# Layer 0 of a two-layer image kernel: two normalising products moved from VectorE to GpSimd

## The chip, the cores and the metric

The kernel runs on one core of one Trainium2 chip. The metric is device time in microseconds (us) of one execution of the whole program: the median of three runs of the kernel before is 8276.61 us (8267.24 to 8282.14).

## The reference, cut to what matters

Two layers, each a mixer and then a small quantised feed-forward network, on an image `x` of shape (2, 96, 96, 96): batch, channel, row, column. The change lies in the mixer of layer 0, in two of its normalisations:

```python
def _ln_c(v, eps=1e-6):                     # over the 96 channels
    m = jnp.mean(v, axis=1, keepdims=True)
    s = jnp.var(v, axis=1, keepdims=True)
    return (v - m) / jnp.sqrt(s + eps)

x = x + _L0_conv_ref(_ln_c(x), ...)
# inside _L0_conv_ref
xz = einsum('bchw,ec->behw', x, in_proj_w)  # xin (192 channels) and a gate z
x_s = grid_sample_bilinear(xin, ...)        # offsets from a 3x3 convolution of xin
...                                         # four directions, each:
    hst = hst * dA + (dt * ut) * bt         # selective scan over windows of 36, 16 states
    y = einsum('bkdn,bkn->bkd', hst, ct)
mu = y.mean(-1); var = ((y - mu) ** 2).mean(-1)            # over 192 channels
y = (y - mu) * rsqrt(var + 1e-05) * ln_gamma + ln_beta
return einsum('bhwd,od->bohw', y * silu(z), out_proj_w)
```

The norm of `x` (the first function) and the norm of `y` (over the 192 channels after the scan) are what the change touches.

## The kernel before

Layer 0 walks over 32 stripes (2 images, 16 stripes of 6 rows, so T = 576 positions, H2 = 288 the half of them). For each stripe there is a front (`_l0_front`, line 488), a scan (`_l0_scan`, 1013, and `_l0_section`, 1055) and a back (`_l0_back`, 936). While stripe n is scanned, the front of stripe n+1 and the back of stripe n-1 are slipped in between.

The front normalises 8 rows of `x` in two column blocks of 384 (`norm`, from line 532): TensorE subtracts the mean (L534), ScalarE squares into `sq` and copies the centred values into `xc` (L538, L539), TensorE averages the squares into the PSUM tile `va` (L542), ScalarE turns them in place into reciprocal deviations by Ln and Exp (L548, L549), and VectorE multiplies `xc` by `va` into `xn` (L552). TensorE then projects `xn` (L557). The rest of the front is the convolution, the interpolation on GpSimd (14 sums and products a stripe, L681 to L687), and the step sizes of the scan, with four GpSimd products each (L810 to L813). The temporaries of the front come from five buffers with the tag "g".

The scan has 64 units for each stripe, 2048 in all. A unit is: TensorE spreads B over the partitions into the PSUM tile `bp` (L1104), VectorE multiplies it by `dur` (L1108), VectorE runs the scan into a state tile `h` in SBUF (L1125), GpSimd multiplies `h` by the replicated C, `cre` (L1130), and TensorE folds the states into `y` (L1143). ScalarE makes the decays `dA` for two units at a time (L1088). There are six state tiles `h`, two `bp` and two `dA`. The first product of every pair of units waits also for the GpSimd product and the fold of the unit whose state tile comes free (`wait` in `unit`).

The back centres `y` (L956 on TensorE; L966 and L967 on ScalarE write the squares `ysq` and the tile `Y`), averages the squares into a PSUM tile `yva`, takes the reciprocal deviation in place on ScalarE (`_power`, L862 and L863), and VectorE multiplies both halves of `Y` by it, 96x576 elements an instruction, two instructions a stripe (L975). GpSimd multiplies `Y` by the gate `zs` (L984), TensorE projects and adds the input (L994, L998), and a feed-forward network follows (`_plan_ffn`), with a VectorE product of its own (L894) and a GpSimd sum at the end (L932). The temporaries of the back, [96, 576] each, come from two buffers with the tag "b".

The order of the instructions is not written out by hand. `_Plan` takes every operation with its engine, a planned cost (`_cost`, by engine and columns, in RATE), its dependences, its buffers and a due time, and lays the operations out in a list order for each engine; `_in_order` then fixes this order. Due times of the scan come from a planned 3.4 us a unit, those of front and back are spread between two such points (`_dues`). Where the plan leaves TensorE idle, it fills in small matmuls without effect (`keep` in `_layer0`, L1188), so many for each gap. An operation that moves from one engine to another changes the plan, and so the order on all engines. Layer 1 follows when layer 0 has ended, with plans of its own.

Of the kernel before, what the change touches and what calls it, by code (L numbers as in the profile page):

```python
# [13 lines left out]
AF = mybir.ActivationFunctionType  # L14
ALU = mybir.AluOpType
# [11 lines left out]
C = 96  # L27
HW = 96
# [4 lines left out]
T = WIN * HW  # L33
H2 = T // 2
# [74 lines left out]
class _Plan:  # L109
# [19 lines left out]
    def op(self, eng, cost, run, r=(), w=(), due=0.0, tab=None, also=(), scan=False, first=False):  # L129
        o = _Op(eng, cost * self.rate.get(eng, 1.0), run, due, tab)  # L130
        o.scan, o.first = scan, first
        ref = lambda t: t if isinstance(t, tuple) else (t, None)
        meets = lambda a, b: a is None or b is None or a == b
        for t, key in map(ref, r):
            o.deps.update(p for p, q in t.writes if meets(key, q))
        for t, key in map(ref, w):
            o.deps.update(p for p, q in t.writes + t.reads if meets(key, q))
        for t, key in map(ref, r):
            t.reads.append((o, key))
        for t, key in map(ref, w):  # L140
            t.writes.append((o, key))
        o.deps.discard(o)
        for t in [x[0] for x in map(ref, list(r) + list(w))] + list(also):
            if t not in o.tiles:
                o.tiles.append(t)
        for t in o.tiles:
            if not t.users and t.tag != "p":
                t.queue.append(t)
            t.users.append(o)
        self.ops.append(o)  # L150
        return o
# [323 lines left out]
def _cost(S, eng, cols):  # L475

    fixed, each = (RATE if S.fine else LOOSE)[eng]
    return fixed + each * cols


def _op(S):
    def op(eng, n, run, r, w, also=(), tab=None, times=1):
        S.op(eng, times * _cost(S, eng, n), run, r, w, also=also, tab=tab)

    return op


def _l0_front(k, P, S, f, x, b, s, at):
# [3 lines left out]
    nc = k.nc  # L492
# [4 lines left out]
    temp = lambda shape, name, skip=0: S.tile(P.front, shape, "g", P.ng, name=name, skip=skip)  # L497
# [4 lines left out]
    def pe(cols, run, r, w, also=()):  # L502
        S.op("pe", _cost(S, "pe", cols), run, r, w, also=also)

    def act(cols, run, r, w, tab=None, times=1):
        S.op("act", times * _cost(S, "act", cols), run, r, w, tab=tab)

    def dve(cols, run, r, w):
        S.op("dve", _cost(S, "dve", cols), run, r, w)
# [17 lines left out]
    pool(8, lambda: nc.gpsimd.memset(xin.ap[:, :, :, 1 : HW + 3 : HW + 1], 0.0), (), (xin,))  # L527
    rows = lambda t, c: t.ap[:, 4 * c : 4 * c + 4, :].rearrange("p r w -> p (r w)")
    N4 = 4 * HW
    xc, sq, xn = temp([C, 8, HW], "axc"), temp([C, 8, HW], "asq"), temp([C, 8, HW], "xn")  # L530

    def norm(c):
        pc, va = ps("axc"), ps("ava")
        pe(N4, lambda: nc.tensor.matmul(  # L534
            pc.ap[:C, :N4], k.less_mean, rows(xt, c), start=True, stop=True), (xt,), (pc,), (xc,))

        def centred():
            nc.scalar.activation(rows(sq, c), pc.ap[:C, :N4], AF.Square)  # L538
            nc.scalar.copy(rows(xc, c), pc.ap[:C, :N4])  # L539

        act(N4, centred, (pc,), ((xc, c), (sq, c)), times=2)
        pe(N4, lambda: nc.tensor.matmul(  # L542
            va.ap[:C, :N4], k.mean96, rows(sq, c), start=True, stop=True),
            ((sq, c),), (va,), (xn,))

        def power():
            v = va.ap[:C, :N4]
            nc.scalar.activation(v, v, AF.Ln, bias=k.eps6[:C])  # L548
            nc.scalar.activation(v, v, AF.Exp, scale=-0.5)  # L549

        act(N4, power, (), (va,), tab="e", times=2)
        dve(N4, lambda: nc.vector.tensor_tensor(  # L552
            rows(xn, c), rows(xc, c), va.ap[:C, :N4], ALU.mult), ((xc, c), va), ((xn, c),))

    def project(half, c):
        pi, n = ps("pi"), PART[half]
# [7 lines left out]
    for c in range(2):  # L564
        norm(c)
# [282 lines left out]
def _dues(S, n0, at):  # L848

    ops = S.ops[n0:]  # L850
    whole, sofar = sum(o.cost for o in ops), 0.0
    for o in ops:
        o.due = at(sofar / whole)
        sofar += o.cost


def _power(k, op, v, eps, out=None):

    v_ = lambda: v.ap[:C, :H2]

    def run():
        k.nc.scalar.activation(v_(), v_(), AF.Ln, bias=eps[:C])  # L862
        k.nc.scalar.activation(v_() if out is None else out.ap, v_(), AF.Exp, scale=-0.5)  # L863

    op("act", H2, run, (), (v,) if out is None else (v, out), tab="e", times=2)
# [70 lines left out]
def _l0_back(k, P, S, f, ffn, res, dst, at):  # L936

    nc = k.nc
    n0 = len(S.ops)
    Y, zs = f.Y, f.zs  # L940
    temp = lambda name: S.tile(P.back, [C, T], "b", 2, name=name)
    ps = lambda name: S.tile(P.ps, [128, 512], "p", P.np, name=name)
    cols = lambda c: slice(c * H2, (c + 1) * H2)

    op = _op(S)
    xr = S.tile(P.back, [C, T], "xr", 1)
    S.op("sp", 1.2, lambda: nc.sync.dma_start(
        xr.ap.rearrange("p (i w) -> p i w", w=HW), res), (), (xr,))
    x1, sq = xr, [temp("ysq"), temp("ysq2")]

    def both(w, src, name, r):

        out = ps(name)

        for half in range(2):
            op("pe", H2, lambda half=half: nc.tensor.matmul(  # L956
                out.ap[:C, :H2], w(half), src(half), start=(half == 0), stop=(half == 1)),
                r, (out,))
        return out

    def centred(c):
        pc = [both(lambda half, h=h: k.less_mean192 if half == h else k.minus_mean192,
                   lambda half: Y.ap[:, half, cols(c)], "yc", ((Y, c),)) for h in range(2)]
        for h in range(2):
            def run(h=h):
                nc.scalar.activation(sq[h].ap[:, cols(c)], pc[h].ap[:C, :H2], AF.Square)  # L966
                nc.scalar.copy(Y.ap[:, h, cols(c)], pc[h].ap[:C, :H2])  # L967

            op("act", H2, run, (pc[h],), ((sq[h], c), (Y, c)), times=2)

    def normed(c):
        va = both(lambda half: k.mean192, lambda half: sq[half].ap[:, cols(c)], "yva",
                  ((sq[0], c), (sq[1], c)))
        _power(k, op, va, k.eps5)
        op("dve", 2 * H2, lambda: nc.vector.tensor_tensor(  # L975
            Y.ap[:, :, cols(c)], Y.ap[:, :, cols(c)],
            va.ap[:C, :H2].unsqueeze(1).to_broadcast([C, 2, H2]), ALU.mult),
            (va,), ((Y, c),))

    for c in range(2):  # L980
        centred(c)
        normed(c)
    for h in range(2):
        op("pool", T, lambda h=h: nc.gpsimd.tensor_tensor(  # L984
            Y.ap[:, h], Y.ap[:, h], zs.ap[:, h], ALU.mult), (zs,), (Y,))

    def project(c):
        pp = ps("pp")

        half = slice(c * HW // 2, (c + 1) * HW // 2)  # L990
        img = lambda t: t.ap.rearrange("p (i w) -> p i w", w=HW)[:, :, half].rearrange(
            "p i (w j) -> p w i j", j=WIN)

        op("pe", H2, lambda: nc.tensor.matmul(  # L994
            pp.ap[:C, :H2], k.ident[:C, :C], img(x1), start=True, stop=False), (Y, zs, (x1, c)), (pp,))
        for n, (w, v) in enumerate(((k.w_outb, zs), (k.w_out, Y))):
            for h in range(2):
                op("pe", H2, lambda n=n, w=w, v=v, h=h: nc.tensor.matmul(  # L998
                    pp.ap[:C, :H2], w[:, h, :], v.ap[:, h, cols(c)],
                    start=False, stop=(n == 1 and h == 1)), (v,), (pp,))  # L1000
        op("act", H2, lambda: nc.scalar.copy(
            img(x1), pp.ap[:C, :H2].rearrange("p (w i j) -> p w i j", i=WIN, j=WIN)),
            (pp,), ((x1, c),))

    for c in range(2):
        project(c)

    x2 = _plan_ffn(k, S, op, ps, temp, P.back, 1, ffn, x1)
    S.op("sp", 1.2, lambda: nc.sync.dma_start(dst, x2.ap), (x2,), ())
    _dues(S, n0, at)  # L1010
# [152 lines left out]
def _layer0(k, tc, a, x, x2d):  # L1163
# [3 lines left out]
    with ExitStack() as st:  # L1167
# [29 lines left out]
        def front(n):  # L1197
            if n < len(stripes):
                t0, t1 = (64 * n - 90) * tau, (64 * n - 12) * tau
                _l0_front(k, P, S, F[n], x, *stripes[n], lambda v: t0 + v * (t1 - t0))  # L1200

        def back(n):
            b, s = stripes[n]
            t0, t1 = (64 * n + 68) * tau, (64 * n + 135) * tau
            _l0_back(k, P, S, F[n], ffn, x[b, :, s * WIN : (s + 1) * WIN, :],
                     x2d[b, :, s * T : (s + 1) * T], lambda v: t0 + v * (t1 - t0))
# [834 lines left out]
```

## Time and profile before

| what | us |
|---|---|
| median of three runs | 8276.61 |
| the profiled execution, its own time | 8276.3 |
| its span in the trace | 8274.5 |
| first scan to last scan of layer 0 | from 149 to 6227 |
| VectorE busy in the span | 7653.1 (92%) |
| TensorE busy | 7337.5 (89%) |
| ScalarE busy | 6308.6 (76%) |
| GpSimd busy | 5188.3 (63%) |
| TensorE clock granted, mean | 0.959 |

PE is TensorE, PEld its weight loads, DVE VectorE, ACT ScalarE, POOL GpSimd. A group's line names the source line, the engine and the operation, output and inputs with their shapes, how often it ran, its busy time and the mean duration of one in ns, and then the idle time of that engine just before, with what ended it. Busy time counts overlapping instructions of an engine once. The shares over the whole span mix two stages: layer 0, in which GpSimd works all the time, and layer 1, after some 6260 us, in which it hardly works.

### The profile page before, as it was taken

Reading aid. Unit: us, or ns where it says so; the run is one execution under the profiler, and the core shown is the slowest. Engines: PE = TensorE matmul, PEld = TensorE weight load, DVE = VectorE, ACT = ScalarE, POOL = GpSimd, SP = SyncE. Lnnn points to the kernel's source line nnn. Section 1 sums busy time; section 2 is a strip of 40 time slices with the busy share of each in tenths; the row PEclk is TensorE's granted clock in tenths of the full one; section 3 lists DMA queues with packets and bytes.
Section 4 is the critical chain, followed back from the end, with each engine's and each line's share of the span. In section 5 each row is a group of like instructions: output and inputs, shape, how many; then the busy total and the mean of one; then the engine's idle time right before and its main releaser. Section 6 shows DMA issues by size and latency. Waiting matters only on the chain. (4 is left out here: it accounts for less than half of the span.)

```text
span 8274.5 us, 124621 instructions
## 1 busy us (share of the span) xinstructions
PE 7337.5 (89%) x46413; PEld 3261.5 (39%) x46413; DVE 7653.1 (92%) x5404; ACT 6308.6 (76%) x10654; POOL 5188.3 (63%) x3835
## 2 busy tenths in 40 slices
PE   7888888888888888888888888988878999989998
PEld 3333344434334333434443433433334223532245
DVE  3999999999999999999999999999996998969988
ACT  5777777778777887877777787778756886778867
POOL 4888888888888888888888888888862000110001
PEclk8999998999999999999999999999999999989999
DMA  3445544544545454454545454454441000110001
GB/s 93 159 156 156 157 151 155 156 151 156 157 153 158 156 166 153 153 159 155 155 150 157 150 157 156 155 159 158 154 132 47 3 3 20 33 47 3 2 22 33
DMA packets 359853, 992.25 MB, mean 120 GB/s; under 512 B 69288, under 2 KB 71680, under 8 KB 359040
## 3 DMA queue, kind: packets, MB, share of 16 engines
q1 hardware_dynamic: 357440, 984.04, 38.3%
q8 instruction: 367, 6.01, 0.3%
q14 instruction: 254, 2.08, 0.1%
q10 hardware_dynamic: 1792, 0.12, 0.0%
HBM read 797.19 MB, written 139.25 MB: 113 GB/s over the span
## 5 line engine op out<-in xcount | busy, mean ns | idle before, releaser
L1130 POOL TENSOR_TENSOR h<-h,cre 128x864 f32<-128x864 f32 x2048 | 3475.2, 1713 | 957.4 <-DVE h L1125 639.7
L1125 DVE TENSOR_TENSOR_SCAN h<-dA,bp 128x864 f32<-128x864 f32 x2048 | 3900.6, 1939 | 51.2 <-PE y L1143 30.6
L1088 ACT ACTIVATE dA<-dlr,A 128x576 f32<-128x576 f32 x3072 | 2157.9, 765 | 892.8 <-DVE h L1125 839.8
L1108 DVE TENSOR_TENSOR bp<-dur,bp 128x864 f32<-128x864 f32 x2048 | 2082.2, 1048 | 187.9 <-PE bp L1104 81.4
L1143 PE MATMUL y<-h,fold 128*32 128x288 f32 (+2 forms) x18432 | 1789.7, 436 | 229.6 <-POOL h L1130 202.1
L1143 PEld LDWEIGHTS y<-h,fold 128*32 128x32 f32 x18432 | 738.8, 114 | 963.4 <-POOL h L1130 674.8
L1503 ACT ACTIVATE pr<-sc 128x960 f32<-128x960 f32 (+1 forms) x1080 | 954.0, 937 | 200.1 <-PE sc L1499 179.2
L1104 PE MATMUL bp<-bt,selb 128*128 128x288 bf16 x2048 | 615.6, 301 | 508.4 <-DVE h L1125 491.2
L1583 DVE TENSOR_TENSOR sums<-sums,pr 128x3840 f32<-128x3840 f32 (+1 forms) x240 | 959.1, 3996 | 55.7 <-ACT pr L1503 33.7
L1675 POOL MEMSET vch<- 96x32 f32 x16 | 2.4, 153 | 1319.7 <-DVE dist L1537 1210.1
L1104 PEld LDWEIGHTS <-selb 128*128 128x128 bf16 x2048 | 198.9, 97 | 1200.9 <-DVE h L1125 1006.3
L1499 PE MATMUL sc<-qH,kH 32*128 32x480 f32 (+1 forms) x3240 | 627.4, 602 | 9.6 <-issue 5.0
L1188 PE MATMUL y<-selb,minus 128*32 128x288 bf16 x3528 | 605.7, 295 | 0.0
L1499 PE MATMUL sc<-q,kH 32*128 32x480 f32 (+1 forms) x1080 | 564.6, 602 | 0.0
L1565 PE MATMUL av<-pr,vT 128*32 128x480 f32 (+1 forms) x4320 | 533.4, 564 | 3.7 <-ACT av L1590 3.5
L1756 DVE SCALAR_TENSOR_TENSOR acc<-vch,lepe_w,acc 96x1152 f32<-96x1152 f32 x320 | 466.2, 1457 | 8.4 <-ACT vch L1691 0.4
L1188 PEld LDWEIGHTS <-minus 128*32 128x32 bf16 x3528 | 298.0, 98 | 225.6 <-issue 131.2
L1499 PEld LDWEIGHTS sc<-qH,kH 32*128 32x128 f32 x3240 | 219.6, 184 | 419.8 <-issue 220.6
L617 PE MATMUL pc<-xin,w_ca 128*128 128x288 f32 x1152 | 365.1, 423 | 1.2 <-ACT xin L560 1.2
L932 POOL TENSOR_TENSOR x<-x,fy 96x576 f32<-96x576 f32 x32 | 52.9, 1653 | 461.4 <-ACT fy L931 372.4
L791 PE MATMUL pt<-xd,w_dt 96*128 96x288 f32 x768 | 280.7, 455 | 7.3 <-ACT r L797 4.4
L810 POOL TENSOR_TENSOR e<-e,du 128x576 f32<-128x576 f32 x192 | 231.1, 1204 | 60.0 <-ACT du L806 59.7
(284 smaller groups left out, 10961.8 us busy)
## 6 DMA issues: line engine op xcount, KB each, us to landing
cre<-c_d SPq DMA_DIRECT2D x1024, 288.0 KB, 3.5
dur<-du_d SPq DMA_DIRECT2D x256, 864.0 KB, 5.6
dlr<-dl_d SPq DMA_DIRECT2D x256, 864.0 KB, 5.1
x<-xs SPq DMA_DIRECT2D x512, 72.0 KB, 2.4
du_d<-du SPq DMA_DIRECT2D x128, 288.0 KB, 2.5
dl_d<-dl SPq DMA_DIRECT2D x128, 288.0 KB, 2.6
du_d<-du SPq DMA_DIRECT2D x128, 144.0 KB, 2.5
dl_d<-dl SPq DMA_DIRECT2D x128, 144.0 KB, 2.4
```

The lines of the kernel that those rows point to most:

```text
L1088: nc.scalar.activation(dA.ap[:, :, blk, :], dlr.ap[:, blk, :].rearrange("p (c n) -> p c n", c=2), AF.Exp, scale=k.A[:, i, kg, h, blk : blk ...
L1104: nc.tensor.matmul(bp.ap[:, :H2], k.selb[:, kk, i, :], f.bc[o].ap[:, toks], start=True, stop=True)
L1108: nc.vector.tensor_tensor(bp.ap[:, : NBL * H2].rearrange("p (b n) -> p b n", b=NBL)[:, ::-1], dur.ap[:, ::-1, toks], bp.ap[:, :H2].unsquee ...
L1125: nc.vector.tensor_tensor_scan(hv, dv, bv, 0.0, ALU.mult, ALU.add)
L1130: nc.gpsimd.tensor_tensor(ht.ap, ht.ap, cre.ap[:, toks].unsqueeze(1).to_broadcast([128, NBL, H2]), ALU.mult)
L1143: nc.tensor.matmul(dst, k.fold, v, start=start, stop=stop)
L1188: nc.tensor.matmul(P.awake.ap[NBL * CB :, T - HEAD + 2 * 72 : HEAD], k.minus[:, :CB], k.selb[:, 0].rearrange("p i m -> p (i m)")[:, : HEAD ...
L1499: nc.tensor.matmul(two[to // 2][:, to % 2, :n], kH[rows, k0 : k0 + 128], q, start=True, stop=True)
L1503: nc.scalar.activation(pr[:, 2 * i : 2 * i + 2, :n], two[i][:, :, :n], AF.Exp, scale=HD**-0.5)
L1565: nc.tensor.matmul((main if s < HEADS else other)[s * HD : (s + 1) * HD, :n], vT[:, blk, hd, :], pr[:, place(s, p), :n], start=at == 0, st ...
L1583: nc.vector.tensor_tensor(both, both, pr[:, :, :, :n], ALU.add)
L1756: S.op("dve", 1.43, lambda: nc.vector.scalar_tensor_tensor(acc.ap, src(), W.lw[:, t : t + 1], acc.ap, ALU.mult, ALU.add), (vch,), (acc,))
```

## The change

In the front, the Exp no longer writes to the PSUM tile but to the SBUF tile of the squares `sq` (which the mean has read by then), and the product is issued on GpSimd, from `xc` and `sq`. `sq` gets a start that is two floats into its buffer. In the back the same is done with `sq[0]` and `Y`; `_power` is written out as a function of its own there. The back's temporaries have three buffers in place of two, and start two floats into theirs.

```diff
-    xc, sq, xn = temp([C, 8, HW], "axc"), temp([C, 8, HW], "asq"), temp([C, 8, HW], "xn")
+    xc, sq, xn = temp([C, 8, HW], "axc"), temp([C, 8, HW], "asq", 2), temp([C, 8, HW], "xn")
...
             nc.scalar.activation(v, v, AF.Ln, bias=k.eps6[:C])
-            nc.scalar.activation(v, v, AF.Exp, scale=-0.5)
-
-        act(N4, power, (), (va,), tab="e", times=2)
-        dve(N4, lambda: nc.vector.tensor_tensor(
-            rows(xn, c), rows(xc, c), va.ap[:C, :N4], ALU.mult), ((xc, c), va), ((xn, c),))
+            nc.scalar.activation(rows(sq, c), v, AF.Exp, scale=-0.5)
+
+        act(N4, power, (), (va, (sq, c)), tab="e", times=2)
+        pool(N4, lambda: nc.gpsimd.tensor_tensor(
+            rows(xn, c), rows(xc, c), rows(sq, c), ALU.mult), ((xc, c), (sq, c)), ((xn, c),))
...
-    temp = lambda name: S.tile(P.back, [C, T], "b", 2, name=name)
+    temp = lambda name: S.tile(P.back, [C, T], "b", 3, name=name, skip=2)
...
-        _power(k, op, va, k.eps5)
-        op("dve", 2 * H2, lambda: nc.vector.tensor_tensor(
+        rs = lambda: sq[0].ap[:, cols(c)]
+
+        def power():
+            nc.scalar.activation(va.ap[:C, :H2], va.ap[:C, :H2], AF.Ln, bias=k.eps5[:C])
+            nc.scalar.activation(rs(), va.ap[:C, :H2], AF.Exp, scale=-0.5)
+
+        op("act", H2, power, (), (va, (sq[0], c)), tab="e", times=2)
+        op("pool", 2 * H2, lambda: nc.gpsimd.tensor_tensor(
             Y.ap[:, :, cols(c)], Y.ap[:, :, cols(c)],
-            va.ap[:C, :H2].unsqueeze(1).to_broadcast([C, 2, H2]), ALU.mult),
-            (va,), ((Y, c),))
+            rs().unsqueeze(1).to_broadcast([C, 2, H2]), ALU.mult),
+            ((sq[0], c),), ((Y, c),))
```

## The prediction, made before the result

> **What bounds the kernel now.** I read the page's slices first: GpSimd is busy to about 6250 us, which is layer 0; after that the changed lines don't run. So only layer 0 matters, and I took the stretch from its first scan to its last (149 to 6227 us) for all further views. The busy times of that stretch:
>
> ```profile
> core 0: us, PE busy (x) PEld busy (x) DVE busy (x) ACT busy (x) POOL busy (x), PEclk, DMA share, GB/s
> 149.00:6227.00 6078.00, 5297.41 (x34108) 2420.51 (x34106) 5896.27 (x4278) 4695.65 (x8119) 5019.07 (x3605) 0.96 0.49 154
> ```
>
> DVE is busy 5896.3 of 6078 us (97%), and idle for 182 us. POOL is busy 83%, PE 87%, of which 605 us are the filling matmuls of L1188. 6078 / 2048 units is 2.97 us a unit. The groups of DVE in this stretch:
>
> ```profile
> L1125 DVE TENSOR_TENSOR_SCAN h<-dA,bp 128x864 f32<-128x864 f32 x2048 | 3900.6, 1939 | 51.2 <-PE y L1143 30.6 <-ACT dA L1088 9.9 <-POOL bot L687 1.6
> L1108 DVE TENSOR_TENSOR bp<-dur,bp 128x864 f32<-128x864 f32 x2046 | 2080.2, 1048 | 137.9 <-PE bp L1104 81.4 <-POOL h L1130 27.8 <-ACT dA L1088 6.3
> L975 DVE TENSOR_TENSOR Y<-Y,yva 96x576 f32<-96x576 f32 x62 | 45.4, 732 | 0.8 <-ACT yva L863 0.8
> L552 DVE TENSOR_TENSOR xn<-axc,ava 96x384 f32<-96x384 f32 x60 | 31.6, 531 | 0.0
> L894 DVE TENSOR_TENSOR fxq<-fxc,fva 96x288 fp8e5<-96x288 f32 x62 | 26.7, 433 | 0.0
> ```
>
> The reader is to see that the two products the change removes hardly ever wait (0.8 us): they stand in a full queue and push the scan back by their own length. Who makes DVE wait, and who makes POOL wait:
>
> ```profile
> DVE bp L1108 <- PE bp L1104: 81.4, 106, 2.6
> DVE h L1125 <- PE y L1143: 30.6, 26, 4.7
> DVE bp L1108 <- POOL h L1130: 27.8, 40, 1.9
> ...
> POOL h L1130 <- DVE h L1125: 639.7, 367, 6.9
> ```
>
> POOL waits for DVE far more than DVE for POOL: POOL is the follower. The chain of waits of the last stripe says the same (products and scans of DVE, no POOL until the scans are over). The groups of POOL that price the new work:
>
> ```profile
> L1130 POOL TENSOR_TENSOR h<-h,cre 128x864 f32<-128x864 f32 x2047 | 3473.5, 1713 | 957.3 <-DVE h L1125 639.7 <-PE y L1143 81.5 <-issue 34.3
> L984 POOL TENSOR_TENSOR Y<-Y,zs 96x576 f32<-96x576 f32 x62 | 74.2, 1203 | 0.0
> L932 POOL TENSOR_TENSOR x<-x,fy 96x576 f32<-96x576 f32 x32 | 52.9, 1653 | 461.4 <-ACT fy L931 372.4 <-DVE acc L1756 59.9 <-ACT fva L862 15.6
> ```
>
> **What the Trainium skill says.** GPSIMD Engine Reference, section 3.1, puts a float32 tensor_tensor at 1.96 times VectorE's time. The trace agrees roughly: 1203 ns for 96x576 on POOL against 732 ns on DVE, 1.64 times. PSUM — Partial Sum Buffer, section "The four PSUM rules", says that GpSimd cannot touch PSUM: so the Exp must write to SBUF before POOL can take the product; in the trace no POOL group has a PSUM operand. SBUF — State Buffer, section "Who interferes with whom", says that a VectorE instruction with two SBUF inputs blocks, or is blocked by, a GpSimd instruction that reads SBUF, and one with a single SBUF input isn't. In layer 0 every DVE product and scan has one input in PSUM, and the scan took 1917 to 1971 ns in all its 2048 runs, with POOL working or not: agrees. The change brings no DVE instruction with two SBUF inputs. ScalarE: Activation LUTs, section "What ACT_TABLE_LOAD costs", has 1283 ns for a load (plus a drain, which I can't see in the trace); the trace shows 1283.
>
> **The change part by part**, against the profiled execution's own time of 8276.3 us (span 8274.5), which is the median of the runs within 0.3 us.
>
> (a) *Removed from DVE.* 64 products of `xn` and 64 of `Y`; 60 and 62 of them are recorded in the stretch, 31.6 + 45.4 = 77.0 us. Neighbours on DVE overlap: the durations add up to 2048 x 1.939 + 2046 x 1.048 + 77.0 + 26.7 = 6218.9 us, the busy time is 5896.3, so each of the 4278 instructions hides 75 ns. Freed: 77.0 - 122 x 0.075 = 68 us. All of it lies on the path, since DVE is full.
>
> (b) *Lost overlap.* A scan that follows straight on its own product can't overlap it. The timeline shows both cases:
>
> ```profile
> 3010.51 3.79 DVE L1125 TENSOR_TENSOR_SCAN h<-dA,bp 128x864 f32<-128x864 f32 x2
> 3014.22 1.04 DVE L1108 TENSOR_TENSOR bp<-dur,bp 128x864 f32<-128x864 f32 x1
> 3015.29 1.95 DVE L1125 TENSOR_TENSOR_SCAN h<-dA,bp 128x864 f32<-128x864 f32 x1
> 3017.16 2.00 DVE L1108 TENSOR_TENSOR bp<-dur,bp 128x864 f32<-128x864 f32 x2
> 3019.07 3.79 DVE L1125 TENSOR_TENSOR_SCAN h<-dA,bp 128x864 f32<-128x864 f32 x2
> 3022.78 2.00 DVE L1108 TENSOR_TENSOR bp<-dur,bp 128x864 f32<-128x864 f32 x2
> ```
>
> A single unit takes 3017.16 - 3014.22 = 2.94 us, a pair 3022.78 - 3017.16 = 5.62, or 2.81 a unit. In the compiled order such scans number 233 before and 278 after, because removed products had stood between the two: 45 x 0.13 = +6 us.
>
> (c) *Added to POOL.* `Y` by the row of L984: 64 x 1.20 = 77 us. A 96x384 product isn't in the trace; between 1203 ns for 576 and 662 ns for a 96x288 product of layer 1 (L1283) it is 0.84: 54 us. Together 131 us, or 4.1 a stripe. From both sides: not under 0.66 a piece for `xn` (the smaller shape), and not over 1.65 for either (L932 in layer 1, where it met other DVE work): 119 to 211 us. POOL idles for 1059 us in the stretch, so the mean has room; what decides is bunching. I added up the order's heaviest runs with these prices: 12 units in a row cost POOL 38.7 us before and 39.9 after at most, against 12 x 2.97 = 35.6 for DVE; 32 units 91.3 and 93.9 against 95. POOL falls some 4 us behind either way, which six state tiles (six units, 17.8 us) cover. Cover that is gone shows as waits of DVE for POOL; those, and the waits for the fold behind it, are 27.8 + 30.6 = 58 us now. POOL's idle share falls from 17.4% to about 14.5%; if waits grow in inverse ratio, 58 x (17.4 / 14.5 - 1) = +12 us. This term is a choice; its ends are -20 (the new order happens to meet fewer waits) and +40.
>
> (d) *A wait moved.* The POOL products wait for ScalarE's Exp, and behind them on POOL stand state products, for which PE's folds and then DVE wait. On DVE the same wait cost 0.8 us in 122 instructions; the plan puts the product behind the Exp. I take zero, hidden by the state tiles; at worst 128 waits of the longest seen there (0.8) make 102 us on POOL, within its idle time.
>
> (e) *ScalarE.* Exp writes SBUF in place of PSUM: 387 ns for 96x288 into PSUM (L863), 387 for the copy of the same shape from PSUM into `Y` in SBUF (L967): zero. The order has 378 table loads against 360: 18 x 1.28 = 23 us on an engine with 1382 idle us there; zero on the path. The PSUM tile comes free a product earlier, the squares' tiles later; the third buffer of the back covers the latter. Zero.
>
> (f) *PE.* 3146 filling matmuls against 3528, 382 fewer of 0.29 us: 110 us less on PE, but they fill gaps only. Zero. SP's queue carries the same DMAs, none is added, and POOL issues none.
>
> (g) *Ends.* Before the first scan, `xn` comes later by 0.84 - 0.55 = 0.3 us. After the last scan the chain runs Exp, product, two gate products: the second Exp ends at 6237.07, two POOL products of 1.2 end by about 6238.65 and the gate by 6241.05, against 6240.30: +0.8 us.
>
> Sum: -68 + 6 + 12 + 1 = -49; 8276.3 - 49 = 8227 us.
>
> **The rivals.**
> *More than that:* the replanned order also meets fewer waits (PE's queue is lighter by the filling). With (c) at -20 and (b) at zero: -68 - 20 + 1 = -87, 8189. For it: 112 of the 182 idle us are waits for PE. Against: nothing was done about them.
> *PE takes over:* the freed time turns into waits for `bp` of L1104, since PE is busy 87% and is the latest releaser already (81.4 us). It would give 8270 to 8280, say 8274. For it: PE's work is unchanged and packed closer. Against: PE waits for DVE's scans before most of these matmuls, and 605 us of its busy time is filling.
> *Slower, by GpSimd's bunching:* the added 131 us lie in the queue ahead of state products, at the places where POOL is already behind (interpolation, step sizes); each delays the release of a state tile, and DVE stops. If all of it reached DVE: -68 + 6 + 131 + 1 = +70, 8346; with three quarters, 8313. It decides from 68 - 7 = 61 us, 47% of the added time. For it: POOL's rows of 1.2 us come in runs. Against: 40 waits for POOL in 2046 products.
> That the change doesn't do what it says is out: the compiled order has 128 DVE instructions fewer and 128 POOL ones more.
>
> **How the numbers follow.** About 0.2% of 8276, 16 us, is what the measurement can tell from no change. Forecast (8200 to 8255) 0.57; more than that 0.16; PE takes over 0.15, of which a third still ends below 8260; slower by bunching 0.12, of which a quarter ends within 16 us. Faster: 0.57 + 0.16 + 0.05 = 0.78; same 0.10 + 0.03 = 0.13; slower 0.09. The range goes from the low end of the second case (8180) into the third case (8278).
>
> **What would show it.** Right: the stretch of the scans is 45 to 90 us shorter, DVE's idle time there stays near 190 us, L975 and L552 appear on POOL at 1.2 and 0.84 us, and layer 1 is as long as before. Wrong: waits of DVE for POOL over 90 us (bunching), for L1104 over 130 (PE), POOL products at twice their price, or scans longer than 1.95 us.

## The result, and the profile after

The changed kernel takes 8160.81 us, the median of four runs (8149.47 to 8167.62), against 8272.03 us for the kernel before in the same comparison: a ratio of 0.9863, 95% interval 0.9845 to 0.988, so 111 us less. The forecast was 8227 us with a range from 8180. The sign was right, the gain was more than twice the 49 us forecast, and the time lies below the range. The profiled execution, the fastest of the four, has a span of 8147.7 us, 126.8 less than the one before.

The line numbers of the changed kernel are six higher from the back on: the product `bp` is L1114, the scan L1131, the state product L1136, the spread L1110, the fold L1149. First the stretch from the first scan to the last, with the busy time of each engine:

```profile
core 0: us, PE busy (x) PEld busy (x) DVE busy (x) ACT busy (x) POOL busy (x), PEclk, DMA share, GB/s
148.00:6095.00 5947.00, 5212.03 (x33725) 2369.59 (x33723) 5821.53 (x4156) 4713.82 (x8137) 5130.13 (x3727) 0.97 0.50 157
```

The stretch is 131 us shorter (6078 before). DVE's busy time fell by 74.7 us (5896.3 before), and its idle time by 56 (181.7 before, 125.5 now). So the gain has two parts of similar size. POOL carries 111 us more. The groups of DVE, and the new ones of POOL, in this stretch:

```profile
L1131 DVE TENSOR_TENSOR_SCAN h<-dA,bp 128x864 f32<-128x864 f32 x2048 | 3900.0, 1939 | 61.4 <-PE y L1149 39.9 <-ACT dA L1094 7.2 <-POOL bot L686 1.7
L1114 DVE TENSOR_TENSOR bp<-dur,bp 128x864 f32<-128x864 f32 x2046 | 2073.4, 1046 | 71.2 <-PE bp L1110 24.1 <-PE y L1149 17.2 <-ACT dA L1094 12.2
L894 DVE TENSOR_TENSOR fxq<-fxc,fva 96x288 fp8e5<-96x288 f32 x62 | 26.8, 432 | 0.0
...
L981 POOL TENSOR_TENSOR Y<-Y,ysq 96x576 f32<-96x576 f32 x62 | 74.6, 1204 | 0.0
...
L552 POOL TENSOR_TENSOR xn<-axc,asq 96x384 f32<-96x384 f32 x60 | 51.8, 864 | 0.0
```

The scan's mean didn't move (1939 ns), and the two products cost POOL what was forecast (1204 and 864 ns, against 1.20 and 0.84). Who makes DVE wait, in us, times and longest, and below it POOL's first wait:

```profile
DVE h L1131 <- PE y L1149: 39.9, 39, 2.9
DVE bp L1114 <- PE bp L1110: 24.1, 44, 1.7
DVE bp L1114 <- PE y L1149: 17.2, 21, 1.7
...
DVE bp L1114 <- POOL h L1136: 2.2, 9, 0.4
...
POOL h L1136 <- DVE h L1131: 507.5, 308, 5.6
```

DVE waited 81.4 us for the spread matmul before and 24.1 now; for POOL's state product 27.8 and 2.2. Both were expected to stay or grow. The wait for the folds grew, from 33.4 to 57.1 (two lines each). So the wait for POOL and for the folds behind it is nearly the same in sum, and the fall of the idle time is as large as the fall of the wait for the spread matmul. Busy time is explained by the products that left. The experiments ask where the 56 us of idle time went.

### The profile page after: what moved, and what is told of

It reads as the page before. It is cut to its first block, busy times and chain, and to the rows that moved or that the text cites. A ratio compares the mean times of both kernels' runs of the same rounds, so it can differ in the third digit from the quotient of the medians.

```text
span 8147.7 us, 123836 instructions
## 1 busy us (share of the span) xinstructions
PE 7250.8 (89%) x46031; PEld 3210.3 (39%) x46031; DVE 7575.8 (93%) x5276; ACT 6328.2 (78%) x10672; POOL 5305.7 (65%) x3963
## 5 line engine op out<-in xcount | busy, mean ns | idle before, releaser
L1136 POOL TENSOR_TENSOR h<-h,cre 128x864 f32<-128x864 f32 x2048 | 3481.2, 1714 | 753.5 <-DVE h L1131 507.5
L1131 DVE TENSOR_TENSOR_SCAN h<-dA,bp 128x864 f32<-128x864 f32 x2048 | 3900.0, 1939 | 61.4 <-PE y L1149 39.9
L1114 DVE TENSOR_TENSOR bp<-dur,bp 128x864 f32<-128x864 f32 x2048 | 2075.4, 1046 | 188.4 <-DMA dur<-du_d 117.3
L1149 PE MATMUL y<-h,fold 128*32 128x288 f32 (+2 forms) x18432 | 1790.0, 434 | 221.7 <-POOL h L1136 198.7
L1149 PEld LDWEIGHTS y<-h,fold 128*32 128x32 f32 x18432 | 725.9, 113 | 974.9 <-POOL h L1136 669.5
L1110 PE MATMUL bp<-bt,selb 128*128 128x288 bf16 x2048 | 613.5, 300 | 458.7 <-DVE h L1131 440.4
L1110 PEld LDWEIGHTS <-selb 128*128 128x128 bf16 x2048 | 197.3, 96 | 1163.0 <-DVE h L1131 956.4
L1194 PE MATMUL y<-selb,minus 128*32 128x288 bf16 x3146 | 552.0, 301 | 0.0
L1194 PEld LDWEIGHTS <-minus 128*32 128x32 bf16 x3146 | 274.0, 100 | 212.5 <-issue 122.3
L932 POOL TENSOR_TENSOR x<-x,fy 96x576 f32<-96x576 f32 x32 | 53.2, 1662 | 461.1 <-ACT fy L931 387.7
L791 PE MATMUL pt<-xd,w_dt 96*128 96x288 f32 x768 | 264.2, 440 | 7.7 <-ACT r L797 4.8
```

Of the source, the lines that this page charges most:

```text
L1110: nc.tensor.matmul(bp.ap[:, :H2], k.selb[:, kk, i, :], f.bc[o].ap[:, toks], start=True, stop=True)
L1114: nc.vector.tensor_tensor(bp.ap[:, : NBL * H2].rearrange("p (b n) -> p b n", b=NBL)[:, ::-1], dur.ap[:, ::-1, toks], bp.ap[:, :H2].unsquee ...
L1131: nc.vector.tensor_tensor_scan(hv, dv, bv, 0.0, ALU.mult, ALU.add)
L1136: nc.gpsimd.tensor_tensor(ht.ap, ht.ap, cre.ap[:, toks].unsqueeze(1).to_broadcast([128, NBL, H2]), ALU.mult)
L1149: nc.tensor.matmul(dst, k.fold, v, start=start, stop=stop)
L1194: nc.tensor.matmul(P.awake.ap[NBL * CB :, T - HEAD + 2 * 72 : HEAD], k.minus[:, :CB], k.selb[:, 0].rearrange("p i m -> p (i m)")[:, : HEAD ...
```

## The experiments

Times are medians; "idle" is DVE's in the stretch from 148 us to the end of the last scan, one profiled execution each. The kernel before was run beside every group, at 8270 to 8282 us, and the ratio is to those runs, taken from all runs and not from the two medians. A difference in us between kernels of two groups is uncertain by these 12 us.

| kernel | us | ratio to before (95%) | DVE busy | idle |
|---|---|---|---|---|
| before | 8272.0 | 1 | 5896 | 183 |
| changed | 8160.8 | 0.9863 (0.9845 to 0.988) | 5822 | 125 |
| e1 old order, product on POOL | 8360.0 | 1.0099 (1.0076 to 1.0122) | 5838 | 332 |
| e2 held plan, product on DVE | 8327.6 | 1.0059 (1.0039 to 1.0079) | 5904 | 247 |
| e3 held plan, product on POOL | 8295.7 | 1.0019 (1.001 to 1.0027) | 5846 | 266 |
| e4 before, less filling | 8276.9 | 1.0004 (0.9993 to 1.0016) | 5896 | 185 |
| e5 front alone | 8253.4 | 0.9997 (0.9982 to 1.0013) | 5868 | 176 |
| e6 back alone | 8212.1 | 0.9932 (0.9919 to 0.9945) | 5849 | 166 |
| e7 before, three temporaries | 8291.2 | 1.0027 (1.0017 to 1.0037) | 5887 | 213 |
| e8 changed, two temporaries | 8246.9 | 0.9975 (0.9964 to 0.9986) | 5833 | 214 |
| e9 before, other order | 8317.0 | 1.0044 (1.0028 to 1.006) | 5893 | 233 |
| e10 before, other order | 8292.9 | 1.0018 (1.001 to 1.0025) | 5889 | 210 |
| e11 changed, other order | 8145.5 | 0.9835 (0.9815 to 0.9855) | 5820 | 124 |
| e12 changed, other order | 8160.6 | 0.9852 (0.9832 to 0.9872) | 5823 | 136 |
| e13 held plan, other order | 8216.6 | 0.9919 (0.9892 to 0.9945) | 5833 | 189 |
| e14 held plan, other order | 8264.2 | 0.9986 (0.9977 to 0.9996) | 5832 | 224 |
| e15 two temporaries, other order | 8324.7 | 1.0058 (1.0037 to 1.0078) | 5834 | 290 |
| e16 two temporaries, other order | 8341.7 | 1.0078 (1.0051 to 1.0104) | 5831 | 310 |
| e17 two temporaries, Y's half twice | 8242.9 | 0.9968 (0.9955 to 0.9981) | 5840 | 202 |
| e18 before, Y's half twice | 8286.5 | 1.0021 (1.0013 to 1.0028) | 5900 | 206 |

The reader is to see that the busy column has two values only, some 5890 with the products on DVE and some 5835 with both on POOL (e5 and e6, with one each, lie between), while idle runs from 124 to 332. The times follow the sum of both. The counts of filling matmuls (3065 to 3692) and of ScalarE's table loads (336 to 380) follow from each plan and differ a little too.

One more thing varies. Each run comes with its mean granted TensorE clock, and in one and the same kernel time and clock go together: of the 35 runs of the kernel before beside e1, the fastest took 8238 us at 0.966, the slowest 8298 us at 0.954. A straight line through the 340 runs of the changed kernel, the experiments and the kernel before beside them, with the mean of each kernel in each group taken off, falls by 39 us for 0.01 of the clock (correlation -0.91). Which of the two follows the other, the runs don't show. Carried along this line to 0.960, and so as estimates, the kernel before lies at 8268 to 8275 us in its five groups, and the changed kernel at 8163 (8163 and 8182 in the two other orders, e11 and e12). So the gain is not one of the clock. Where this bears on a reading, the clocks are given below.

### The same order, another engine (e1); another order, the same engine (e2)

e1 keeps the plan of before and changes only what is issued. The reciprocal deviations go to tiles that are free at that place:

```diff
-            nc.scalar.activation(v, v, AF.Exp, scale=-0.5)
+            nc.scalar.activation(rows(xn, c), v, AF.Exp, scale=-0.5)
...
-        dve(N4, lambda: nc.vector.tensor_tensor(
-            rows(xn, c), rows(xc, c), va.ap[:C, :N4], ALU.mult), ...
+        dve(N4, lambda: nc.gpsimd.tensor_tensor(          # planned as before
+            rows(xn, c), rows(xc, c), rows(xn, c), ALU.mult), ...
```

(and the same in the back with `sq[0]`). PE and SP have the old order, instruction for instruction.

> The order of the kernel before, instruction for instruction on every engine, but GpSimd runs the two products at the places where VectorE's stood (ScalarE's Exp writes to SBUF, the planned hold of the PSUM tile unchanged). Theory A (freed VectorE time is all that the change is worth, whatever the order): the old order keeps most of the gain, 95 to 115 us under the kernel before. Theory B (the gain is 75 us of freed time and some 50 us of a better new order): 55 to 80 us under. Theory C (in the old order the GpSimd products come too early or too late and make waits): under 40 us.

It took 8360 us, 78 over before: theory C, and more than C said. DVE was freed of 58 us and idled 149 more. DVE's waits in the same view:

```profile
DVE bp L1114 <- PE bp L1110: 159.9, 168, 4.1
DVE h L1131 <- PE y L1149: 48.4, 46, 5.0
DVE bp L1114 <- POOL h L1136: 42.7, 37, 2.8
```

The wait for the spread matmul is twice as long (159.9 us in 168 cases, 81.4 in 106 before). Taking these waits one by one, by the matmul that filled most of each on PE, 82 us lie with folds (28 before) and 18 with the projection of `xn` (L557; 5 before). The folds' matmuls waited 270 us for POOL's state products, 200 before; the matmuls and weight loads of L557 waited 21 us for the product that is now on POOL, and 9 before for the one on VectorE. This fits a chain in which POOL comes later, the matmuls that need it come later, and the spread matmuls that the order puts behind them come later still; no run takes the chain apart. So moving the products in the order of before loses. Two things blur the size. The mean clock was 0.951, against 0.959 beside it, which by the line above goes with some 30 of the 78 us. And without the start two floats in, both products were slower, 1000 and 1402 ns against 864 and 1204, 21 us of POOL time in all.

e3 is the changed kernel, except that the plan lists the PSUM tile of the variance among the product's inputs, so that its slot is held until then:

```diff
-            rows(xn, c), rows(xc, c), rows(sq, c), ALU.mult), ((xc, c), (sq, c)), ((xn, c),))
+            rows(xn, c), rows(xc, c), rows(sq, c), ALU.mult), ((xc, c), (sq, c), va), ((xn, c),))
...
-            ((sq[0], c),), ((Y, c),))
+            ((sq[0], c), va), ((Y, c),))
```

e2 has the same plan, but ScalarE's Exp writes to PSUM and VectorE multiplies.

> The plan believes that GpSimd runs the products (and that the PSUM tile is held until then), but VectorE runs them. Theory A: as the kernel before, within 15 us, since VectorE has the old work. Theory B: 30 to 60 us under the kernel before, from the order alone. Theory C: slower than before by 10 to 40 us, since the products come into a VectorE queue that has no room planned for them.

> The changed kernel, but its plan holds the PSUM tile of the variance until the GpSimd product has run, as the VectorE product held it before. Theory P (PSUM tiles that come free a product earlier let TensorE's spread matmuls run in time): most of the 50 us beyond the freed time is lost, 30 to 55 us over the changed kernel. Otherwise: within 20 us of the changed kernel, either way, as for any new order.

e2 was 46 us over before (theory C, a little more than it said), e3 14 us over. Between these two only the engine of the products and the place that Exp writes to differ, and with POOL the kernel is 32 us faster, 0.4%: DVE's busy time is 58 us less, its idle time 19 more. So in one and the same order about half of the 68 us that I had counted comes back; at equal clock (0.961 for e2, 0.957 for e3) it would be an estimated 50 us. And e3 is 135 us over the changed kernel, far more than the 30 to 55 of theory P, although its instructions are the same but for 190 more filling matmuls and 4 fewer table loads: the hold costs through the order that the plan then finds.

### Fewer filling matmuls (e4)

```diff
-SPARE, SHARE, STEP = 0.15, 0.8, 0.15
+SPARE, SHARE, STEP = 0.15, 0.715, 0.15
```

> The kernel before in its own order, with 3176 filling matmuls in place of 3528 (the changed kernel has 3146). Theory F (fewer filling matmuls stand ahead of the spread matmuls, for which VectorE waited 81 us before and 24 after): 20 to 50 us under the kernel before. Otherwise: within 10 us of it, or slower if the granted clock falls.

No difference in time, and the wait for the spread matmul stayed:

```profile
DVE bp L1108 <- PE bp L1104: 81.1, 107, 3.2
```

The time alone would not settle it, since the mean clock was lower (0.955 against 0.959, which by the line above goes with some 14 us). The wait does, in one trace each: in the order of before, the filling is not what made those matmuls late, and theory F has fallen.

### One part alone (e5 to e8)

e5 has the hunk of the front alone, e6 that of the back with its temporaries; e7 and e8 change only the number of the temporaries:

```diff
-    temp = lambda name: S.tile(P.back, [C, T], "b", 2, name=name)                # e7: before
+    temp = lambda name: S.tile(P.back, [C, T], "b", 3, name=name, skip=2)
...
-    temp = lambda name: S.tile(P.back, [C, T], "b", 3, name=name, skip=2)        # e8: changed
+    temp = lambda name: S.tile(P.back, [C, T], "b", 2, name=name, skip=2)
```

> Only the norm of x is changed (product on GpSimd, Exp to SBUF, variance's PSUM tile free after the Exp); the back is that of before. Theory Q (each part brings its freed time and its earlier free PSUM tile): 40 to 65 us under the kernel before, and front and back together make the whole gain of 112. Theory O (what counts is which waits a new order happens to meet): anything from 60 us under to 40 us over, and the parts don't add up.

> Only the norm of y is changed, with the three back temporaries; the front is that of before. Theory Q: 50 to 75 us under the kernel before. Theory O: anything from 60 under to 40 over, and not what the front leaves of 112.

> The kernel before with three back temporaries that start two floats into their buffers, both products still on VectorE. Theory T (the third buffer lets the plan spread the back, and that takes the waits for the spread matmuls away): 30 to 60 us under the kernel before. Otherwise within 20 us of it.

> The changed kernel with two back temporaries in place of three. Theory T: 30 to 60 us over the changed kernel. Otherwise within 20 us of it; theory O leaves both open.

The front alone brings nothing that can be measured (its 22 runs spread from 8226 to 8323 us), the back alone 0.7%, both 1.4%: the parts don't add up. The third temporary alone makes the kernel before 0.3% slower; taken from the changed kernel it costs 86 us. In these orders it is worth something only together with the move. That fits theory T for the changed kernel alone, and theory O for all four: a new order is drawn each time. One order for each case can't tell.

### How far an order alone moves the time (e9 to e12)

The plan's cost of a scan or of a state product is changed by 5 ns. Nothing else differs but the order, and the filling and table loads that follow from it.

```diff
-        S.op("dve", 1.87, scan, ...                # e9 on before, e11 on changed
+        S.op("dve", 1.865, scan, ...
...
-        S.op("pool", 1.7, times_c, ...             # e10 on before, e12 on changed
+        S.op("pool", 1.695, times_c, ...
```

> The kernel before, whose plan takes 1.865 us for a scan in place of 1.87: same instructions and buffers, another order. Theory O (an order drawn anew changes the waits by tens of us): 15 to 60 us off the kernel before, in either direction. Theory S (the order is sound whatever the small print; the 56 us beyond the freed time belong to the change): within 12 us of it.

> The kernel before, whose plan takes 1.695 us for the GpSimd product of a state in place of 1.7. Theory O: 15 to 60 us off the kernel before, in either direction. Theory S: within 12 us.

> The changed kernel, whose plan takes 1.865 us for a scan. Theory O: the changed kernel had a good draw, so this one comes out slower, 20 to 70 us over it, about 40 to 90 us under the mean of the kernels before with their draws. Theory S: within 12 us of the changed kernel.

> The changed kernel, whose plan takes 1.695 us for the GpSimd product of a state. Theory O: 20 to 70 us over the changed kernel. Theory S: within 12 us of it.

The kernel before becomes 0.4% (e9) and 0.2% (e10) slower by its draws; e10's 11 us lie within what theory S allowed. The changed kernel stays within 16 us, and one draw is faster (8145.5 us, the fastest kernel of this study). So theory O fails for the changed kernel: its low idle time (125, 124, 136) is no luck of one order. The three orders of before idle 183, 233 and 210. The mean over three orders, 209 against 129, is a gain of 80 us in idle time, beside 71 in busy time. The profiled executions of the changed kernel ran at a clock of 0.963 to 0.966, those of before at 0.957 to 0.959, which by the line above goes with some 25 us of the sum. Of theory O the scatter remains: about 0.4% for the kernel before.

The two waits that fell in the first traces are low in the other orders of the changed kernel as well. Before, in e9 and e10:

```profile
DVE bp L1108 <- PE bp L1104: 55.5, 87, 2.6
DVE bp L1108 <- POOL h L1130: 20.7, 31, 1.7
...
DVE bp L1108 <- PE bp L1104: 56.6, 86, 1.9
...
DVE bp L1108 <- POOL h L1130: 31.7, 38, 2.4
```

Changed, in e11 and e12:

```profile
DVE bp L1114 <- PE bp L1110: 42.7, 67, 2.6
...
DVE bp L1114 <- POOL h L1136: 13.2, 21, 1.7
...
DVE bp L1114 <- PE bp L1110: 29.2, 47, 1.7
...
DVE bp L1114 <- POOL h L1136: 7.7, 14, 1.7
```

Over three orders each, the mean wait for the spread matmul is 64.5 us before and 32.0 changed, that for the state product 26.7 and 7.7.

### New orders for the hold and for the temporaries (e13 to e16)

The same two edits of the planned costs, on e3 and on e8.

> The kernel with the planned hold of the variance's PSUM tile, in another order (1.865 us planned for a scan). Theory P (the planned hold itself costs the waits): again over 8230 us, 70 us or more over the changed kernel. Theory O (the first such order was a bad draw): within 40 us of the changed kernel, about 8160 to 8200.

> The same with 1.695 us planned for the GpSimd product of a state. Theory P: over 8230 us. Theory O: 8160 to 8200.

> The changed kernel with two back temporaries, in another order (1.865 us planned for a scan). Theory T (with products on GpSimd the squares' tile is held longer, and the third buffer takes that hold out of the plan): again 8225 us or more. Theory O: within 40 us of the changed kernel, about 8160 to 8200.

> The same with 1.695 us planned for the GpSimd product of a state. Theory T: 8225 us or more. Theory O: 8160 to 8200.

With the hold: 8296, 8217, 8264 us, 56 to 135 over the changed kernel's 8161. With two temporaries: 8247, 8325, 8342, 86 to 181 over. e13 lies between the two theories, so the size of the hold is uncertain; but six orders of six are slower than all three of the changed kernel, and no interval of their ratios to before meets one of the changed kernel's. At a clock of 0.960 the six are estimated at 8224 to 8344 us, the three at 8163 to 8182. Both are causes: without either, about half of the gain or more goes. Without the third temporary the move made the kernel slower in two of three orders.

### A second buffer for the first half of Y (e17, e18)

The traces with two temporaries show a stop of DVE that the three orders of the changed kernel don't have. From the timeline of e16, one stop near the middle of a stripe (start, duration, instruction, and in brackets the idle time before it):

```profile
4850.05 1.06 DVE L1114 TENSOR_TENSOR bp<-dur,bp 128x864 f32<-128x864 f32 x1 [0.66 <-PE bp L1110]
...
4860.91 0.65 PE L1004 MATMUL pp<-Y,out_proj 96*96 96x288 f32 x2
...
4862.20 0.56 ACT L1045 COPY Y<-y 96x504 f32<-96x504 f32 x1
4862.77 0.66 ACT L1047 COPY Y<-y 32x72 f32<-32x72 f32 x3
4863.48 2.86 PE L1149 MATMUL y<-h,fold 128*32 128x288 f32 x30 [1.93 <-ACT Y L1047]
...
4864.78 1.95 DVE L1131 TENSOR_TENSOR_SCAN h<-dA,bp 128x864 f32<-128x864 f32 x1 [13.66 <-PE y L1149]
```

The back of the last stripe still projects from Y (L1004) when the scan has filled `y`; ScalarE copies it out only then, PE's folds wait for the copy, the six state tiles fill up, and DVE stops for 13.7 us. There were six and eight such stops of 9.9 us or more in e15 and in e16, two in e8, none in the changed kernel. They are not peculiar to the changed kernel with two temporaries: one order of the kernel before (e9) has four, e5 two, and an order with three temporaries and the hold (e14) two. Theory H was that this hand-over of the single tile Y is why the third temporary counts. The tile is split in halves, the first gets two buffers, and the normalising product is issued half by half:

```diff
-    f.Y = S.tile(P.hand, [C, 2, T], "Y", 1)
+    f.Y = [S.tile(P.hand, [C, T], f"Y{h}", 2 - h) for h in range(2)]
```

> The changed kernel with two back temporaries, but with the first half of Y in a tile of its own that has two buffers (the second half keeps one; the GpSimd product is issued by halves, some 0.24 us more a stripe). Theory H (with two temporaries the back comes late, so Y comes free late for the next stripe's first half, TensorE's folds stop at units 32 to 47 and VectorE behind them): VectorE's idle time in units 32 to 47 falls under 25 us (66, 147 and 192 us in the three orders with two temporaries) and the time to 8150 to 8210 us. Theory T (the third temporary is needed for another reason): still 8235 us or more, with the idle time in another place or the same.

> The kernel before, with the same two buffers for the first half of Y and its VectorE product issued by halves (4 x 0.43 in place of 2 x 0.73 us a stripe: 9 us more in all). Theory H: the 48 us of VectorE's idle time in units 32 to 47 fall under 25, the time is 10 to 40 us under the kernel before. Otherwise: 0 to 30 us over it, for the halves and another order.

DVE's wait for the folds in e16, in e8 (which has the planned costs of e17), and then in e17:

```profile
DVE h L1131 <- PE y L1149: 189.8, 48, 16.6
```

```profile
DVE h L1131 <- PE y L1149: 93.6, 40, 20.3
```

```profile
DVE h L1131 <- PE y L1149: 69.9, 53, 2.7
```

The long stops are gone (longest 2.7 us). But idle time in units 32 to 47 fell to 55 us only, not under 25, and 8243 us is no better than the best of the three orders with two temporaries. In e18 the idle time in these units is what it was (47 us, 46 before), and the time is 15 us over before, at a lower clock (0.952 against 0.959, which would go with more than that). So the hand-over explains the long stops, as far as the one order of e17 tells. What e15 and e16 idle more than e8 (76 and 96 us) lies in these units, but the split tile was not run in their orders. The hand-over does not explain the remaining 80 us to the changed kernel, nor the idle time of the kernel before. Theory H has fallen as the whole answer.

## Why the prediction was wrong

(a) and (b), DVE's busy time: -68 + 6 = -62 forecast, -75 measured. Right in kind, 13 us short: DVE's durations in the stretch add up to 80 us less (6219 before, 6139 now), since the `bp` products got 4 us shorter besides, and the time that neighbours hide fell by 5.5 us (323.0 to 317.5), where (a) and (b) together took 15 as lost. That all of the freed time lies on the path is not borne out: between e2 and e3, in one order, some half of it came back.

(c) The prices on POOL were right, 132 us for all the products (64 x 1.204 + 64 x 0.864, at the measured means) against 131. Wrong was the choice that waits grow with POOL's load, +12 us: DVE's wait for POOL's state product went from 27.8 to 2.2, and with the folds behind it from 61 to 59. A share of idle time said little here, where the order of the queue is planned.

(d) Zero was right: POOL never waited for ScalarE at a product in the stretch (0.0 in both groups).

(e) This is the step that failed. It read "The PSUM tile comes free a product earlier, the squares' tiles later; the third buffer of the back covers the latter. Zero." ScalarE's time was rightly costed at nothing, with 18 more table loads: DVE waited 16 us for `dA` before and 19 now. But the two buffers were not nothing: when the plan holds the PSUM tile until the product again, 56 to 135 us are lost (e3, e13, e14), and without the third buffer 86 to 181 (e8, e15, e16). I had looked only for waits that the changes would add on the chip, and named the third buffer as a cover for one of them. It was the lighter limits in the plan that let a better order be found, and the idle time fell by 56 us where 12 more were forecast; DVE's wait for the spread matmul, which the sum left as it was, fell from 81.4 to 24.1 us. For the profiled execution, 78 us under the forecast, the two differences add up to the miss: 13 + 68 = 81 us, less some 3 us that the end of layer 0 and layer 1 took more than (g) allowed. The median is 66 us under the forecast; the profiled execution was the fastest of four.

(f) Zero is what e4 shows, at a somewhat lower clock. (g) The chain from the last scan to the end of the gate came out as sized, 14.1 us against 13.3. What was not counted came behind it: from the end of the last scan to the end of the last L932 it is 36.1 us against 32.9.

The rivals: "more than that" (8189 us) was the nearest and had 0.16; its mechanism, fewer waits by a new order, is what happened, but the reason it gave, lighter filling, does not show in e4, where less filling left the wait as it was. "PE takes over" and "bunching" are what e1 shows, where the order stayed old: DVE's wait for the spread matmul rose to 159.9 us and that for the state product to 42.7.

What stays open is how the planned hold turns into waits: how a slot that the plan frees later moves the folds that stand in front of spread matmuls. The kernels show that it does, in three orders each, not by which operation. Open is also what the start two floats into the buffers brings to the time: the kernels with the hold or with two temporaries have it and are slow, so it is not enough, but the changed kernel was not run without it. And whether the granted clock is a cause or a companion of the time is not known.

## What to carry to other kernels

In a kernel whose order comes from a plan, an operation's move between engines is three changes: its time, the buffers it holds or releases, and the order drawn from both. Price each; here the buffers' part was of the size of the freed time or larger, and the move without the new order (e1) was a loss. The three orders of one kernel lay 0.3 to 1.0% apart here, so before reading a difference of one per cent or less as a cause, draw two more orders of both kernels with a neutral edit of the plan, and look at the clocks of the runs.

## What the runs showed of the hardware that was not expected

A start two floats into a buffer goes with faster GpSimd products. The product of `Y` by `sq[0]`, in place, took 1402 ns in e1, where `sq[0]` starts at its buffer's start, and 1203 in the changed kernel, where it starts two floats in; the product into `xn` took 1000 ns from `xc` and `xn` in e1, where it overwrites its second input, and 863 from `xc` and `sq`, two floats in. For the product of `Y`, first e1 and then the changed kernel:

```profile
L981 POOL TENSOR_TENSOR Y<-Y,ysq x64: 1392/1402/1432, 360.4 to 6328.4; 96x576 f32<-96x576 f32 x64
```

```profile
L981 POOL TENSOR_TENSOR Y<-Y,ysq x64: 1188/1203/1222, 372.8 to 6105.4; 96x576 f32<-96x576 f32 x64
```

The three numbers are least, median and most; the ranges of 64 instructions each don't meet. Other addresses may have moved with the edit, and for `xn` the operands differ too, so the start is the known difference, not a proven cause.
